# Attention values of the 65 last keys with the operands exchanged: weights stationary, keys moving, and a transpose per head

## The chip, the core and the metric

The kernel runs on one core of a Trainium2 chip. The metric is the device time of one execution in microseconds (us); the median of several runs counts. The engines are called as in the profile: PE (TensorE matmuls) with its weight loads PEld, DVE (VectorE), ACT (ScalarE), POOL (GpSimd) and SP (SyncE, which issues most DMAs). PSUM is the memory that PE writes; it has 8 banks of 128 partitions x 512 f32.

## The reference

A gated cross-attention block and a feed-forward block with eight low-rank experts, all in f32. The change lies in the values `v` of the cross-attention: 4 batches, 256 queries, 1601 keys, 8 key/value heads of 128, 32 query heads.

```python
def _L0_xattn_ref(query, kv, Wq, bq, Wkv, bkv, Wo, bo):
    q = (query @ Wq + bq).reshape(B, L, NKV, G, HDIM)
    k_, v_ = jnp.split(kv @ Wkv + bkv, 2, axis=-1)
    k = k_.reshape(B, Lk, NKV, HDIM)
    v = v_.reshape(B, Lk, NKV, HDIM)
    scores = jnp.einsum('blkgd,bmkd->bkglm', q, k) * scale
    attn = jax.nn.softmax(scores, axis=-1)
    o = jnp.einsum('bkglm,bmkd->blkgd', attn, v).reshape(B, L, NHEAD * HDIM)
    return o @ Wo + bo
...
x = x + jnp.tanh(g_xattn[0]) * _L0_xattn_ref(_layernorm(x, axis=-1), ctx_4096, ...)
x = x + jnp.tanh(g_ffn[0]) * _L0_ffn_ref(_layernorm(x, axis=-1), ...)
```

1601 keys are 12 blocks of 128 and a rest of 65. The 65 are the subject here.

## The kernel before

**Groups and windows.** The work is cut into groups, one for each batch, key/value head and block of 128 queries (`run_group`, L1783). In a group PE makes the scores of 13 key blocks (`score_unit`, L1246, PSUM tile `sc`), which ACT copies to SBUF (L1255), and in between, for the group before, the product of the exponentials with the values (`av_unit`, L1337, tile `av`). DVE folds maxima and sums and subtracts, ACT takes the exponentials (L1285, L1288). Between two groups lies a window (`window`, L1800), in which PE does the other work: queries (`pxq` and the like), keys (`pxk`), values (`pxv`) and output products (`po`, L472, evacuated by ACT at L477).

**The planner.** The order on PE, DVE and ACT is written out by the Python code, which keeps a clock for each of them with a planned cost for each step. A step is a tuple of cost, what it waits for, the function that issues it, and whether it takes a PSUM bank. Steps that must follow each other form a `Task` with a due window. Tasks with a `chain` share `RATE` = 9700 ns of a window by their cost: in L1811, `t.credit = t.cost() * max(min(1, left / max(cost, 1)), 0)`, and a step is taken while half its cost is within the credit. In the window where a task is due its credit is unlimited. Among the steps that may be taken, the one that is ready first goes first (L1822). Between scores, `short_tasks` (L1749) takes steps of up to 4 x 108 ns where they are ready and three banks are free. `act(ns)` adds a piece to ACT's clock and says when its result is there (200 ns for each of the two signals). `bank` takes a PSUM bank from the planner's list, and `give` returns it.

**The values of a pair of heads.** `pair_steps` (L971) makes two heads at once with Strassen-Winograd's seven products, in which the weights' blocks and sums of them (`A11` ... `S4`, 128 x 128 for each `a(slot, c)`) meet blocks of the context and sums of those. For the values, the context is stationary and the weights move (L1015), so that keys come to lie on partitions, as `av` needs them. There are two parts of 384 keys in each half, seven steps of 1344 ns in each part. The 65 keys of the rest do not go through the seven products. `tail` (L1124) makes them directly: for each head `f` four matmuls, with the 65 keys (`cols`, from `tail_cols`) stationary and the weights moving, into 65 partitions x 128 of one bank (`ptv`, L1128); then ACT copies each head's part to block `FULL` of `v_t` (L1136). `tail` is a task of its own beside the two parts, with the same due window and chain. When all steps of the pair are over (`over`, L1141), the weights of the next keys are loaded by SP.

**How often.** 4 batches x 4 pairs of heads, less the first pair, which takes another way: 15 times. Each f32 matmul appears in the trace as two records (each with its weight load), each f32 transpose as one.

**Names of the diff.** `REST` = 65, `P` = `HDIM` = 128, `NC` = 4, `FULL` = 12, `BLOCK_COST` = 224, `TR_COST` = 108 (ns in the plan). `small` is a pool of small SBUF tiles, `ident` the 128 x 128 identity. `banks` and `second` are dictionaries that live as long as the pair's steps; `done` holds the planned time at which a named result is there.

Of the kernel before, what the change touches and what calls it, by code (L numbers as in the profile page):

```python
# [10 lines left out]
F32 = mybir.dt.float32  # L11
# [4 lines left out]
P = 128  # L16
NHEAD = 32
NKV = 8
HDIM = 128
# [8 lines left out]
def flamingo_kernel(  # L28
# [51 lines left out]
    nc = tc.nc  # L80
    B, L, D = x.shape
    LK = ctx_kv.shape[1]
    NC = D // P
# [5 lines left out]
    FULL = KT - 1 if rows[-1] < P else KT  # L89
# [14 lines left out]
    REST = rows[-1] if FULL < KT else 0  # L104
# [8 lines left out]
    small = ctx.enter_context(tc.tile_pool(name="small", bufs=4))  # L113
# [10 lines left out]
    done = {}  # L124
# [7 lines left out]
    def act(ns, ready=None):  # L132
        clock["a"] = max(clock["a"], clock["now"] + SEM if ready is None else ready) + ns
        return clock["a"] + SEM
# [76 lines left out]
    def bank(name):  # L211
        free.remove(min(free))
        return ps.tile([P, 512], F32, tag="bank", name=name)
# [4 lines left out]
    ident = const.tile([P, P], F32, name="ident")  # L218
# [33 lines left out]
    TR_COST = 108  # L252
    BLOCK_COST = 224
# [612 lines left out]
    qT_t, kT_t, v_t = {}, {}, {}  # L866
# [64 lines left out]
    def first_k_steps(b):  # L931

        steps = sum(pair_steps("k", b, 0, lambda: next_weights("v", b, 0)), [])
        return steps
# [36 lines left out]
    def pair_steps(kind, b, hp, then=None):  # L971
# [4 lines left out]
        nm = f"{kind}_{b}_{hp}"  # L976
        h0 = 2 * hp
        banks = {}
        second = {}

        def a(slot, c):
            return w_t[kind, b, hp][:, slot, c, :]
# [130 lines left out]
        def tail_cols(f):  # L1113

            rest, tt = rest_t[b], T_t[b][1]
            if f == 0:
                return [(rest[:, c, :], A11, c) for c in range(2)] + [
                    (rest[:, 2 + c, :], A12, c) for c in range(2)
                ]
            return [(rest[:, c, :], S1, c) for c in range(2)] + [  # L1120
                (tt[:, c, :], A22, c) for c in range(2)
            ]

        def tail():  # L1124
            bk = bank(f"pt{nm}")
            for f in range(2):
                for j, (cols, slot, c) in enumerate(tail_cols(f)):
                    nc.tensor.matmul(  # L1128
                        bk[:REST, f * HDIM : (f + 1) * HDIM],
                        cols,  # L1130
                        a(slot, c),
                        start=j == 0,
                        stop=j == NC - 1,
                    )
            for f in range(2):
                nc.scalar.copy(v_t[b, h0 + f][:REST, FULL], bk[:REST, f * HDIM : (f + 1) * HDIM])  # L1136
                t = act(250)
            give(t)
            over()

        def over():  # L1141
            left[0] -= 1
            if not left[0]:
                done["pair", kind, b, hp] = clock["now"]
                if then is not None:
                    then()
# [12 lines left out]
        parts = [[step(i, s, n) for i in (1, 2, 6, 7, 5, 4, 3)] for s, n in cols]  # L1159
        if REST and not wide:  # L1160
            ready = [("T", "kv", b), ("w", kind, b, hp)]
            parts.append([(2 * NC * BLOCK_COST, ready, tail, True)])
        left = [sum(len(p) for p in parts)]
        return parts

# [688 lines left out]
    def q_steps(b, h, i):  # L1854

        hp = h * NL + i

        def then():

            if (b, hp) == (0, 0):  # L1860
                next_weights("q", 0, 2)
            elif hp + 1 < NHEAD // 2 and (b, hp) != (0, 1):
                next_weights("q", b, hp + 1)

        return pair_steps("q", b, hp, then)[0]
# [110 lines left out]
    for hi, (b, h) in enumerate(heads):  # L1976
        pair, coming = (b, h // 2), next_pair(b, h // 2)
        nxt = heads[hi + 1] if hi + 1 < len(heads) else None
        for l in range(NL):
# [26 lines left out]
            if coming is not None and (h % 2, l) == (0, 1):  # L2006
                cb, cp = coming
                if cb == b:
                    then = lambda c=coming: next_weights("v", *c)
                    steps = sum(pair_steps("k", cb, cp, then), [])  # L2010
                else:
                    steps = first_k_steps(cb)
                tasks.append(Task(steps, (hi | 1) * NL + (NL - 1) * (cb == b), now))
# [66 lines left out]
```

## Time and profile before

| | us |
|---|---|
| median of 3 runs (2532.05 to 2533.65) | 2532.07 |
| the profiled execution's own time | 2532.2 |
| its span, first to last instruction | 2530.4 |
| PE busy in it | 2521.6 |
| DVE busy | 2175.3 |
| ACT busy | 1263.6 |
| `ptv` matmuls, L1128: 180 and 60 records | 22.1 and 9.0 |
| the copies of `ptv`, L1136: 30 | 0.262 each (median) |

A line of groups gives the line of the code, the engine and operation, the tile written and the tiles read, for PE the shape of the stationary operand (rows x columns) and of the result, the number of records, then the busy time, the mean of one in ns and the idle time before them. Records of matmuls overlap, so that busy times of neighbours do not add up; the chain of waits gives each piece its own share. In a matmul's line the first tile read is the moving one and the second the stationary one. A line of the order of time has the start, the length, the engine, the line, the operation and how many records were merged into it.

### The profile page before, as it was taken

What the parts mean: (1) busy time and instruction counts of PE and PEld (TensorE: products, weight loads), DVE (VectorE), ACT (ScalarE), POOL (GpSimd) and SP (SyncE); (2) the same over time, 40 slices, a digit from 0 to 9 for tenths busy, and PEclk for the clock granted to TensorE, in tenths of its full rate; (3) what the DMA queues carried; (4) which work ended last, traced back from release to release, by engine and by line L of the source; (5) the groups of instructions that cost most, each with busy time, mean ns of one, the idle gap of its engine ahead of it and who ended that gap; (6) DMA issues with size and microseconds to landing.
All of it is one profiled execution on the core that took longest, in us unless ns stands there. A gap on an engine that the chain in (4) does not pass through costs nothing.

```text
span 2530.4 us, 27018 instructions
## 1 busy us (share of the span) xinstructions
PE 2521.6 (100%) x9199; PEld 1493.8 (59%) x9199; DVE 2175.3 (86%) x3323; ACT 1263.6 (50%) x2062; POOL 208.8 (8%) x271
## 2 busy tenths in 40 slices
PE   9999999999999999999999999999999999999999
PEld 7557566565555656555665565756656565555544
DVE  4999898898899989999878887878788888889886
ACT  2545454545455554555545454545455455555551
POOL 1000000001001000110010000000000100000100
PEclk9999999999999999999999999999999999999999
DMA  5646857669666543224255535455532222221211
GB/s 170 143 92 130 146 123 118 151 110 246 80 92 99 85 81 74 71 71 152 58 98 100 98 77 96 109 81 110 154 80 65 82 54 67 67 63 44 71 34 50
DMA packets 300136, 246.24 MB, mean 97 GB/s; under 512 B 180533, under 2 KB 256341, under 8 KB 296158
## 3 DMA queue, kind: packets, MB, share of 16 engines
q1 hardware_dynamic: 267278, 211.71, 36.6%
q0 software_dynamic: 32192, 32.55, 8.8%
q8 instruction: 72, 1.18, 0.2%
q14 instruction: 66, 0.54, 0.1%
q10 hardware_dynamic: 528, 0.26, 0.0%
HBM read 147.96 MB, written 96.49 MB: 97 GB/s over the span
## 4 chain that ended last, share of the span: by engine, by line
PE 98%; DVE 1%; DMA 0%; ACT 0%; issue 0%; SPq 0%; ACTq 0%
PE sc L1246 28%; PE av L1337 27%; PE pxv L1015 6%; PE pxk L1004 6%; PE pxq L1004 4%; PE pox L472 4%; PE pyv L1015 3%; PE pyk L1004 3%; PE pyq L1004 2%; PE poy L472 2%; PE pzv L1015 2%; PE pzk L1004 2%; PE pzq L1004 1%; PE ptv L1128 1%; PE poz L472 1%; PE py L1581 1%
## 5 line engine op out<-in xcount | busy, mean ns | idle before, releaser
L1246 PE MATMUL sc<-qT,kT 128*128 128x512 f32 (+1 forms) x1664 | 775.9, 592 | 0.0
L1337 PE MATMUL av<-p,v 65*128 65x512 f32 x1640 | 765.5, 592 | 0.5 <-ACT p L1288 0.5
L1255 ACT COPY p<-sc 65x512 f32<-65x512 f32 x820 | 478.4, 586 | 572.8 <-PE sc L1246 549.0
L1337 PEld LDWEIGHTS av<-p,v 65*128 65x128 f32 x1640 | 311.2, 190 | 384.3 <-issue 380.1
L1246 PEld LDWEIGHTS sc<-qT,kT 128*128 128x128 f32 (+1 forms) x1664 | 308.1, 186 | 375.6 <-issue 349.5
L1285 DVE TENSOR_TENSOR p<-p,mb 65x512 f32<-65x512 f32 x442 | 482.4, 1136 | 0.3
L1288 ACT ACTIVATE p<-p 65x512 f32<-65x512 f32 x442 | 422.3, 990 | 31.0 <-DVE p L1285 29.7
L1181 DVE TENSOR_TENSOR mx<-mx,p 128x1024 f32<-128x1024 f32 x252 | 308.1, 1223 | 146.3 <-ACT p L1255 141.7
L478 POOL DMA_DIRECT2D kept_x<-po x210 | 182.6, 925 | 2039.8 <-ACT po L477 1864.4
L1181 DVE TENSOR_TENSOR sm<-sm,p 128x1024 f32<-128x1024 f32 x252 | 307.6, 1221 | 42.0 <-ACT p L1288 32.0
L1004 PE MATMUL pxq<-xq,wq 128*128 128x256 f32 x512 | 131.2, 379 | 0.0
L1049 ACT ACTIVATE kT<-pxk,biasT 128x384 f32<-128x384 f32 (+1 forms) x120 | 58.1, 509 | 126.5 <-PE pxk L1004 126.0
L1004 PEld LDWEIGHTS pxq<-xq,wq 128*128 128x128 f32 x512 | 92.4, 189 | 32.1 <-issue 15.8
L1049 ACT ACTIVATE qT<-pxq,biasT 128x256 f32<-128x256 f32 x64 | 30.4, 474 | 148.8 <-PE pxq L1004 148.8
L1175 DVE TENSOR_TENSOR mx<-p,p 128x1024 f32<-128x1024 f32 x63 | 76.9, 1221 | 31.6 <-ACT p L1255 31.4
L1004 PE MATMUL pxk<-T,wk 128*128 128x417 f32 (+1 forms) x240 | 90.4, 499 | 0.0
L1015 PE MATMUL pxv<-wv,ctxT 128*128 128x128 f32 x720 | 90.2, 275 | 0.0
L1015 PE MATMUL pxv<-wv,T 128*128 128x128 f32 x720 | 90.2, 275 | 0.0
L1004 PE MATMUL pxk<-ctxT,wk 128*128 128x417 f32 (+1 forms) x240 | 90.0, 499 | 0.0
L1015 PEld LDWEIGHTS pxv<-wv,ctxT 128*128 128x128 f32 x720 | 86.4, 192 | 4.2 <-issue 3.8
L1015 PEld LDWEIGHTS pxv<-wv,T 128*128 128x128 f32 x720 | 86.4, 192 | 4.2 <-issue 3.8
L1052 ACT COPY v<-pxv 128x384 f32<-128x384 f32 x90 | 43.0, 478 | 83.4 <-PE pxv L1015 83.1
(273 smaller groups left out, 2779.5 us busy)
## 6 DMA issues: line engine op xcount, KB each, us to landing
kept_x<-po POOLq DMA_DIRECT2D x210, 128.0 KB, 4.8
wo<-kept_wo SPq DMA_DIRECT2D x22, 1024.0 KB, 7.8
kept_q<-wq SPq DMA_DIRECT2D x16, 896.0 KB, 4.3
wq<-kept_q SPq DMA_DIRECT2D x16, 896.0 KB, 5.1
space<-kept_wo SPq DMA_DIRECT2D x22, 512.0 KB, 3.9
wk<-kept_k SPq DMA_DIRECT2D x11, 896.0 KB, 4.8
wv<-kept_v SPq DMA_DIRECT2D x11, 896.0 KB, 4.6
ctxT<-kept_ctx SPq DMA_DIRECT2D x12, 801.0 KB, 11.8
```

The source lines that it names most:

```text
L472: nc.tensor.matmul(bk[:, :HD], left[i]()[:, c, :], blk[:, c, :], start=first and c == 0, stop=c == 1, skip_group_check=True,)
L478: nc.gpsimd.dma_start(x2_kept[b, l, d], part, accum_op=ALU.add)
L1004: nc.tensor.matmul(bk[:, :n], a(SLOT[i], c), operand(i, c, s, n), start=first and c == 0, stop=c == 1, skip_group_check=True,)
L1015: nc.tensor.matmul(bk[:, t * HDIM : (t + 1) * HDIM], operand(i, c, s + t * P, P), a(SLOT[i], c), start=first and t == 0 and c == 0, stop=c ...
L1049: nc.scalar.activation(dst, src, AF.Identity, bias=bias_of(kind, h0 + f))
L1175: nc.vector.tensor_tensor(acc, p[first], p[first + 1], op)
L1181: nc.vector.tensor_tensor(acc, acc, p[j], op)
L1246: nc.tensor.matmul(sc[:r, :], kT_t[b, h][:, key_col(i) : key_col(i) + r], qT_t[b, h][:, :, l * P : (l + 1) * P], start=True, stop=True,)
L1255: nc.scalar.copy(p[:r, k, :], sc[:r, :])
L1285: nc.vector.tensor_tensor(p, p, m, ALU.subtract)
L1288: nc.scalar.activation(p, p, AF.Exp, scale=scale)
L1337: nc.tensor.matmul(av, v_t[b, h][:r, i, :], p_t[key][j][:r, k, :], start=(j == 0 and k == 0), stop=(j == NPAIR - 1 and k == len(pairs[j]) ...
```

## The change

`tail` exchanges the operands: the weights `a(slot, c)` are stationary and the 65 keys move, so the result has the 128 value features on partitions and 65 keys along the free axis, 130 columns for both heads. ACT copies it to a new SBUF tile of 128 x 130 (`vr`). A second step, `tail_turn`, transposes each head's 128 x 65 on PE into the free half of the same bank, and ACT copies the two results of 65 x 128 to `v_t` as before. The bank is returned after that. In the plan the task now has two steps: 2 x 4 x 124 ns for the product (before 2 x 4 x 224), and 2 x 108 ns for the turn, which waits for the copy.

```diff
         def tail():
-            bk = bank(f"pt{nm}")
+            banks["t"] = bk = bank(f"pt{nm}")
             for f in range(2):
                 for j, (cols, slot, c) in enumerate(tail_cols(f)):
                     nc.tensor.matmul(
-                        bk[:REST, f * HDIM : (f + 1) * HDIM],
+                        bk[:, f * REST : (f + 1) * REST],
+                        a(slot, c),
                         cols,
-                        a(slot, c),
                         start=j == 0,
                         stop=j == NC - 1,
                     )
+            second["t"] = small.tile([P, 2 * REST], F32, tag="vr", name=f"vr_{nm}", bufs=1)
+            nc.scalar.copy(second["t"], bk[:, : 2 * REST])
+            done[nm, "t"] = act(230)
+            over()
+
+        def tail_turn():
+            bk = banks["t"]
             for f in range(2):
-                nc.scalar.copy(v_t[b, h0 + f][:REST, FULL], bk[:REST, f * HDIM : (f + 1) * HDIM])
+                nc.tensor.transpose(
+                    bk[:REST, (2 + f) * HDIM : (3 + f) * HDIM], second["t"][:, f * REST : (f + 1) * REST], ident
+                )
+            for f in range(2):
+                nc.scalar.copy(
+                    v_t[b, h0 + f][:REST, FULL], bk[:REST, (2 + f) * HDIM : (3 + f) * HDIM]
+                )
                 t = act(250)
             give(t)
             over()
...
         if REST and not wide:
             ready = [("T", "kv", b), ("w", kind, b, hp)]
-            parts.append([(2 * NC * BLOCK_COST, ready, tail, True)])
+            parts.append([(2 * NC * 124, ready, tail, True), (2 * TR_COST, (nm, "t"), tail_turn)])
```

## The prediction

> **What bounds the kernel now.** I read the table of engines first, then the chain of work that ended last, then the groups by line with their shapes kept apart, and last the order of time around one of the places that the change touches.
>
> ```profile
> PE 2521.6 (100%) x9199; PEld 1493.8 (59%) x9199; DVE 2175.3 (86%) x3323; ACT 1263.6 (50%) x2062; POOL 208.8 (8%) x271
> ...
> PE 98%; DVE 1%; DMA 0%; ACT 0%; issue 0%; SPq 0%; ACTq 0%
> ```
>
> PE is busy for the whole span and 98% of the chain is PE. What a change does to the time is therefore what it adds to or takes from PE's own stream, at full price, plus any wait that it brings into that stream. The granted clock is 1.00, so rows from different places can be compared.
>
> The chain in order of time shows one place of the change, in the pieces from 244 to 249 us (start, length, what):
>
> ```profile
> 244.19 1.34 PE pyv L1015 x12
> 245.53 1.34 PE pxv L1015 x12
> 246.87 1.75 PE ptv L1128 x16
> 248.62 0.86 PE pox L472 x4
> ```
>
> `ptv` is the product for the last 65 keys of one pair of heads. It has 8 matmuls in the program and 16 records, two for each f32 matmul. It takes 1.75 us, 0.109 us a record. The line occurs 240 times, so there are 15 such places, 26.2 us in all, 1% of the span. No more than that is at stake.
>
> **What a record costs.** Each record is a weight load (PEld) and a matmul (PE). The forms tell which of the two sets the pace:
>
> ```profile
> L1015 PE MATMUL pxv<-wv,ctxT 128*128 128x128 f32 x720 | 90.2, 275 | 0.0
> L1015 PEld LDWEIGHTS pxv<-wv,ctxT 128*128 128x128 f32 x720 | 86.4, 192 | 4.2 <-issue 3.8
> L1128 PEld LDWEIGHTS ptv<-wv,rest 128*65 128x65 f32 x180 | 20.1, 138 | 0.0
> ```
>
> A matmul moves its columns at 0.83 ns a column: the 512-column form lasts 592 ns, the 128-column one 275 (317 ns for 384 columns). A weight load behaves alike: 192 ns for 128 columns against 138 for 65 is 54 ns for 63 columns, 0.86 ns a column. So 128 columns occupy either side for about 107 ns and 65 for about 55. In `pxv` both sides are 128 wide and the pace is 1.34 us / 12 = 0.112 us, not the sum of the two, so load and move overlap and the longer one counts. In `ptv` now the load is 65 wide and the move 128: 0.109 us.
>
> **The swap of the operands.** Afterwards the weights stand (128 columns to load) and the keys move (65). The longer side goes from the move to the load and stays 128 columns wide. No row before has a 65-column move under a 128-column f32 load, so I bound it. The nearest row comes behind four transposes that move 8 columns each, where a score product finds nothing to hide its load:
>
> ```profile
> 2391.61 0.70 PE L1246 MATMUL sc<-qT,kT 128*128 128x512 f32 x1
> ...
> 2391.61 0.30 PEld L1246 LDWEIGHTS sc<-qT,kT 128*128 128x128 f32 x2
> ```
>
> That matmul lasts 0.70 us where its form means 592 ns, 0.105 us more, and two loads of 0.19 end within 0.30 us, so they start 0.11 us apart. A 128-column load that no move covers is paid in full. Under a 65-column move (55 ns) half of it is covered and the pace should be the load's, 0.107 to 0.112 us. I take 0.110: 16 x 0.110 = 1.76 us a place, +0.01 on 1.75. The bounds of this range are -0.04 (0.107) and +0.04 (0.112). The far bound is the four small transposes themselves:
>
> ```profile
> L259 PE MATMUL pt_base<-ident,base 8*128 8x8 f32 x4 | 0.4, 207 | 0.0
> ...
> 2391.27 0.32 PEld L259 LDWEIGHTS pt_base<-ident,base 8*128 8x128 f32 x4 [0.76 <-issue]
> ```
>
> Their loads start (0.32 - 0.14) / 3 = 0.06 us apart. A transpose's load of 128 columns lasts 140 ns, like 65 columns of an ordinary one, which is why this row is not the nearest. If 0.062 held, a place would take 0.99 us, 0.76 less.
>
> The Trainium skill ("TensorE: Matmul & The Clock Gate", LDWEIGHTS) speaks against the change: by it the load goes by its columns, 107 ns for 128, whatever is moved; the swapped product would then take 1.71 us, an estimate, and gain almost nothing. The same page (The mechanism, under packing) has a load overlap a running matmul only where the row groups differ. The 0.112 us of `pxv`, where both use all rows, contradicts this; by that rule load and move would add to 162 ns before and after alike, an estimate, and the product would neither gain nor lose.
>
> **The two transposes.** Each place gains two transposes, with 65 weight columns and 128 moving ones. The chain has the nearest row, between two ordinary products:
>
> ```profile
> 28.30 0.44 PE pt_x L259 x4
> 28.73 3.46 PE pv L955 x16
> ```
>
> 0.44 / 4 = 0.109 us each, and the product behind them keeps its usual 0.216 us a record: a 128-column move covers the next load. 2 x 0.109 = 0.22 us a place. They are single records, so there are no more than 30 of them.
>
> **The copies on ACT.** A copy of 128 x 130 out of PSUM is added, ahead of the two of 65 x 128 (262 ns each now); about 0.27 us, 15 times, 4 us of an engine that is 50% busy. I cost it at nothing. Every time before, the copies start some 0.04 us behind the end of the product's last record, as here (that record ends at 412.90 + 0.60 = 413.50 us):
>
> ```profile
> 413.54 0.42 ACT L1136 COPY v<-ptv 65x128 f32<-65x128 f32 x2 [1.27 <-PE ptv L1128]
> 414.40 0.47 ACT L477 ACTIVATE po<-pox,gates 128x256 f32<-128x256 f32 x1 [0.44 <-PE pox L472]
> ```
>
> ACT stands idle before them and 0.44 us after them. The first added wait is this copy's on the product: behind it in ACT's queue are the evacuations of the output products and the next exponentials. The second is PE's: the transposes wait for the copy, some 0.35 us after the product's end (0.04 and the copy, and a little for the semaphore). What hides it is the planner's rule that a step is taken by when it is ready: the turn counts as ready 630 ns later (200 + 230 + 200), and other steps stand ready, output products of 0.86 us at every one of the 15 places. If that cover were gone, PE would stand for about 0.5 us a place: 0.16 for the product's drain (a record's 273 ns over its pace of 109), 0.04, the copy and its signal. The bank stays held until the turn, some microseconds longer. PE's waits on other engines total only some 5 us in the whole span, so I put that at nothing as well; its price would show as a wait of PE's on an evacuation by ACT.
>
> **The moved step.** The product's planned cost falls from 1792 to 992 ns, 1208 with the turn. The planner gives a chain of steps a share of each window; for the value steps it is 9700 / 20024 = 0.484 (before 9700 / 20608 = 0.471). The product gets 585 ns of credit and needs half its first step, 496, to be taken; before it had 843 and needed 896. So it should move one window earlier, behind the six `pxv`/`pzv` steps, with the turn in that window or among the next scores. PE does the same work. One window grows by 1.8 us and the other, at the shortest 12.9 us (7 value products, the product, two output products), shrinks to 11.1. Windows of 9.5 us (from 787.01 to 796.48 us: six key products, two output products) already pass with no idle PE, so DVE keeps up. The next weights' load on SP is issued when the chain is over, now up to 1.8 us earlier, and it is used 30 us later (issued at 248.65, first product at 278.55 us). No DMA is added; POOL's queue keeps its order.
>
> **Sum.** A place: +0.01 and +0.22 = +0.23 us. 15 places: +3.4 us on the profiled execution's 2532.2 (its span of 2530.4 and 1.8 around it); the median is 2532.07, 0.1 below. Forecast 2535.5 us, 0.13% slower, which is within the 0.2% (5.1 us) that a measurement of this kernel can tell from no change. Its own range is 2532.5 to 2538: the product's bounds give 15 x (-0.04 to +0.04) = -0.6 to +0.6, the shift of windows perhaps 2 either way, judged by PE's stalls of 0.5 to 0.8 us at single places.
>
> **Rivals.** First, the short move sets the pace and the load hides: 0.062 us a record. 15 x (-0.76 + 0.22) = -8.1 us, 2524.0. The pace of the small transposes speaks for it; the uncovered load of 0.105 us and the loads' 0.86 ns a column speak against it. Chance 0.10.
>
> Second, the transposes come before their copy and PE waits: 0.5 us at each place on top of the sum, 15 x (0.23 + 0.5) = +11, 2543. It is slower beyond the limit from 0.11 us of mean wait on (1.7 / 15). For it: PE runs late on its plan, which counts 992 ns for about 1760, and ACT is in order, so an exponential that waits for DVE would hold the copy. Against it: an output product of 0.86 us stands ready at every place. With shorter waits at some places, and with stalls of DVE in the changed windows, chance 0.26, from 2537 to 2543.
>
> Third, that the change does not do what it says, in that the pair's two products are no shorter and the turn costs its 0.22 us, is the forecast itself. Chance 0.64.
>
> **How the numbers follow.** Within 0.2% holds the forecast, less a little at its upper end and with a few gains: 0.62. Slower 0.28, faster 0.10. The range 2531.5 to 2541 leaves out the first rival and the far end of the second.
>
> **What would show it.** The product should take 1.7 to 1.8 us a place in the chain, with weight loads near 190 ns. About 1.0 us would make the first rival right. Thirty transposes of 272 ns must follow an output product or a score, not the product. A group of PE waits on ACT's new copy would be the second rival. A product that still stands behind the last `pxv` would make the moved step wrong, at no cost in time.

## The result, and the profile after

The changed kernel takes 2538.56 us (median of 14 runs, 2536.87 to 2541.15) against 2532.27 (14 runs of the kernel before beside them, 2531.62 to 2535.46): a ratio of 1.0024, 95% interval 1.0016 to 1.0032, 6.3 us slower. The profiled execution took 2539.2 us, its span is 2537.4.

The tables of engines and of the chain, in the page of the changed kernel:

```profile
PE 2526.5 (100%) x9229; PEld 1498.0 (59%) x9229; DVE 2176.3 (86%) x3323; ACT 1264.6 (50%) x2077; POOL 208.7 (8%) x271
...
PE 99%; DVE 0%; ACT 0%; DMA 0%; issue 0%; SPq 0%; ACTq 0%
```

PE has 30 records more, the transposes, and ACT 15, the new copies. PE still sets the end. The first place of the change, in the chain in order of time (start, length, what):

```profile
204.72 1.73 PE ptv L1128 x16
206.46 0.92 PE poy L472 x4
207.38 0.86 PE pox L472 x4
...
212.16 0.22 PE ptv L1143 x2
```

The product takes 1.73 us where it took 1.75, so the swap gained next to nothing. The output product behind it takes 0.92 where its kind takes 0.86 (by the starts of the records it is 0.05 more). The two transposes take 0.22 and stand 5.7 us behind the product's end, between scores (11.6 us at three of the 15 places). The product stands where the plan now takes it, one window earlier (204.72 us, before 246.87). The forms of the groups show why there is no gain (matmuls, then weight loads):

```profile
L1128 PE MATMUL ptv<-rest,wv 128*128 128x65 f32 x180 | 21.8, 271 | 0.0
...
L1128 PEld LDWEIGHTS ptv<-rest,wv 128*128 128x128 f32 x180 | 21.3, 192 | 0.0
```

The loads have grown from 138 to 192 ns. The matmuls move 65 columns and still last 271; that each waits for its load is tested below.

That explains some 4 of the 6.3 us. The rest shows in PE's waits, by what it waited for (total, times, longest in us):

```profile
PE pox L472 <- DVE space L450: 3.0, 1, 3.0
PE warm L1910 <- DVE ones L1907: 1.1, 1, 1.1
PE pt_ctx L259 <- DMA ctx<-in_ctx_dram: 1.0, 1, 1.0
```

One output product waits 3.0 us for DVE's sums (`space`), where the kernel before waits 0.6 us. The wait at `warm` is in the kernel before too. The one on the first load of the context, near the start, comes and goes (a second profile of the changed kernel has none, one of another kernel below 1.2 us) and is no part of the change. In the order of time PE stands at the output product, and what follows is stretched:

```profile
1104.57 1.81 PE L472 MATMUL pox<-space,space 128*128 128x256 f32 x4 [3.03 <-DVE space L450]
1106.18 4.22 PE L1350 MATMUL av<-p,v 128*128 128x512 f32 x7
```

In the kernel before, the same four records last 1.13 us and the seven behind them 3.17 instead of 4.22:

```profile
1100.06 1.13 PE L472 MATMUL pox<-space,space 128*128 128x256 f32 x4 [0.61 <-DVE space L450]
1101.03 3.17 PE L1337 MATMUL av<-p,v 128*128 128x512 f32 x7
```

So 0.7 and 1.05 us, 1.7 in all, are stretching. The table by stretches of the changed kernel (PE, PEld, DVE, ACT and POOL busy, then the granted clock, and last what DMA moved) says what happened:

```profile
1095.00:1101.00 6.00, 6.00 (x16) 2.60 (x14) 5.89 (x9) 1.37 (x3) 0.00 (x0) 1.00 0.01 3
1104.50:1108.50 4.00, 3.93 (x7) 2.29 (x8) 3.53 (x6) 0.47 (x1) 0.90 (x1) 0.57 0.00 0
1109.00:1115.00 6.00, 6.00 (x44) 5.04 (x43) 5.19 (x12) 0.60 (x2) 0.00 (x0) 1.00 0.11 16
```

The granted clock is 0.57 in the 4 us behind the wait and 1.00 before and after them; in single microseconds it is 0.50 from 1105 to 1108 us. The Trainium skill ("TensorE: Matmul & The Clock Gate", the table of goals under "Why this matters for your kernels") says the same: PE should not stand for more than about 3 us. The wait of 3.03 us here was enough; the one of 0.61 before was not.

DVE's order of time shows where the wait comes from. In the kernel before, around this group, whose first score is at 1080.13 us:

```profile
1069.11 0.67 DVE L1193 TENSOR_REDUCE quadm_sm<-sm 128x16 f32<-128x512 f32 x1
...
1081.02 0.23 DVE L1313 RECIPROCAL quadm_sm<-quadm_sm 32x16 f32<-32x16 f32 x1
...
1099.13 0.42 DVE L450 TENSOR_TENSOR space<-oT 128x256 f32<-128x256 f32 x1
```

and in the changed kernel, whose group begins at 1082.21:

```profile
1087.09 0.68 DVE L1206 TENSOR_REDUCE quadm_sm<-sm 128x16 f32<-128x512 f32 x1
...
1098.21 0.23 DVE L1326 RECIPROCAL quadm_sm<-quadm_sm 32x16 f32<-32x16 f32 x1
...
1103.64 0.42 DVE L450 TENSOR_TENSOR space<-oT 128x256 f32<-128x256 f32 x1
```

The end of the earlier group's sums has moved back: the reduction from 11 us ahead of this group's first score to 5 us behind it, the reciprocal from the head of this group's work into its middle. The sums for the output product come 4.5 us later, and 2.1 of these are PE's own delay: DVE is 2.4 us later against PE. The operations are the same; the plan took them in another order.

### The profile page after: what moved, and what is told of

Read it like the earlier page. It is cut to its first block, busy times and chain, and to the rows that moved or that the text cites. A ratio compares the mean times of both kernels' runs of the same rounds, so it can differ in the third digit from the quotient of the medians.

```text
span 2537.4 us, 27121 instructions
## 1 busy us (share of the span) xinstructions
PE 2526.5 (100%) x9229; PEld 1498.0 (59%) x9229; DVE 2176.3 (86%) x3323; ACT 1264.6 (50%) x2077; POOL 208.7 (8%) x271
## 4 chain that ended last, share of the span: by engine, by line
PE 99%; DVE 0%; ACT 0%; DMA 0%; issue 0%; SPq 0%; ACTq 0%
PE av L1350 28%; PE sc L1259 28%; PE pxv L1015 6%; PE pxk L1004 6%; PE pxq L1004 4%; PE pox L472 4%; PE pyv L1015 3%; PE pyk L1004 3%; PE pyq L1004 2%; PE poy L472 2%; PE pzk L1004 2%; PE pzv L1015 2%; PE pzq L1004 1%; PE ptv L1128 1%; PE poz L472 1%; PE py L1594 1%
```

## The experiments

The theory: the 6.3 us are PE's own work at 15 places, about +0.25 us each, and one wait with the clock behind it, brought by the new order. The rivals: all of it is PE's own work, or all of it is the order. All times are medians beside the kernel before on the same chip, with the ratio and its 95% interval.

**The product kept in its old window.** Only the planned costs differ from the changed kernel:

```diff
-            parts.append([(2 * NC * 124, ready, tail, True), (2 * TR_COST, (nm, "t"), tail_turn)])
+            parts.append([(2 * NC * BLOCK_COST, ready, tail, True), (0, (nm, "t"), tail_turn)])
```

> The exchanged product and the transposes stay, but the plan counts the product at 1792 ns as before and the turn at 0, so that the product stays in the window in which it stood before; DVE's order is then nearly that of before. Theory (two parts: PE's own work at each of the 15 places, and a wait of PE on DVE's sums of the output product that comes from the new order): the product takes 1.73 us a place, the two transposes 0.22 and the product behind the exchanged one 0.05 more, so +0.25 us a place, +3.8 in all: 2536.1 us (2535.3 to 2537.0), clock 1.000, and PE's wait on 'space' under 1 us as before. Rival 'all of it is PE's own work': no different from the changed kernel, 2538.5. Rival 'all of it is the order': 2532.3, as before.

2536.02 us against 2532.39, +3.6 (1.0016, interval 1.0007 to 1.0025). The clock in the profile is 1.0 and the wait 0.6 us. This is the change without its shift of windows, and the rival "all of it is the order" falls, since the interval lies above 1. The chain has 1.74 us for the product, 0.92 for the output product behind it and 0.22 for the transposes.

**The plan alone.** The old operands and copies, with the changed kernel's two planned steps; the second one issues the copies:

```diff
-            parts.append([(2 * NC * BLOCK_COST, ready, tail, True)])
+            parts.append([(2 * NC * 124, ready, tail, True), (2 * TR_COST, (nm, "t"), tail_turn)])
```

> The product and the copies of the kernel before (keys stationary, no transposes), in the plan of the changed kernel: a step of 992 ns that is taken one window earlier, and a second one of 216 ns that issues the two copies. DVE's order is that of the changed kernel. Theory (two parts): PE's wait on 'space' near 1100 us grows from 0.8 to about 3 us and the granted clock falls behind it, so +2 to +4 us: 2534.3 to 2536.3. Rival 'all of it is PE's own work': 2532.3. Rival 'all of it is the order': 2538.5.

2536.89 against 2532.39, +4.5 (1.0020, 1.0012 to 1.0029), 0.6 above the theory's upper end. PE waits 3.0 us on `space`, and in its profile 1.9 us more on sums of the queries. A kernel that computes exactly what the one before does, with the same instructions, loses 4.5 us where the change lost 6.3. So the rival "all of it is PE's own work" falls too. Taken alone, this run leaves the order's rival standing (2538.5 is inside the interval); that one fell with the run before.

**Without the transposes**, in the old window:

```diff
-            for f in range(2):
-                nc.tensor.transpose(
-                    bk[:REST, (2 + f) * HDIM : (3 + f) * HDIM], second["t"][:, f * REST : (f + 1) * REST], ident
-                )
...
+                nc.scalar.copy(v_t[b, h0 + f][:REST, FULL], second["t"][:REST, :HDIM])
```

> As the kernel with the product in its old window, but the 30 transposes are left out: the two copies read the untransposed tile, so the values of the 65 last keys are not the reference's. Theory: the transposes cost their 0.109 us each and nothing else, 30 x 0.109 = 3.3 us less than with them, 2532.9 us; what is left over the kernel before is the exposed load behind the product, +0.5 us. Rival (a turn costs more, by a switch between transposes and products or a wait on the copy): 2 us or more below that, or the kernel with the transposes at 2538 and this one at 2533.

2532.97 against 2532.39 (1.0004, 0.9995 to 1.0013), 3.05 us below the kernel with them. The transposes cost 0.10 us each and nothing besides.

**Half the keys moved**, in the old window. The two copies that fill the tile are not shown:

```diff
-                        bk[:, f * REST : (f + 1) * REST],
+                        bk[:, f * 33 : (f + 1) * 33],
                         a(slot, c),
-                        cols,
+                        cols[:, :33],
```

> As the kernel with the product in its old window, but only 33 of the 65 keys move in each matmul; two copies fill the tile with them twice, so the values of the last 32 keys are not the reference's. Theory (the load of 128 columns sets the pace): the product keeps 1.73 us a place, 0.108 us a record. Rival (the move sets the pace, or load and move add): 32 columns less at 0.83 ns are 27 ns a record, 0.43 us a place, 1.3 us a place and 6.4 us less in all.

2537.05 in its one run, 1.0 above the kernel with 65 keys; its profile has a wait of 1.2 us on the first load of the context, which the other's has not. The rival's 6.4 us less did not come. In its chain:

```profile
246.96 1.71 PE ptv L1128 x16
248.67 0.94 PE pox L472 x4
```

With 33 columns the product and the output product behind it take 2.65 us together, with 65 columns 2.66: what moves does not count. What the product saves at its last record (0.03) the next one pays: its second record starts 0.30 us behind its first, with 65 columns 0.27, and in the kernel before 0.22. The less is moved, the less of the load behind it is covered.

**Half the columns loaded**, in the old window, with 65 keys moving. The two copies are again not shown:

```diff
-                        bk[:, f * REST : (f + 1) * REST],
-                        a(slot, c),
+                        bk[:64, f * REST : (f + 1) * REST],
+                        a(slot, c)[:, :64],
```

> As the kernel with the product in its old window, with 65 keys moving, but only 64 of the 128 weight columns are loaded in each matmul; the 64 features of a head are copied twice, so the values of the 65 last keys are not the reference's. Theory (the load sets the pace): both sides are now about 54 ns, so the record falls from 0.108 us to 0.06, the product from 1.73 to about 0.97 us a place, 11 us less in all. Rival (load and move add, or a record has a floor of 0.1 us): no less than 0.1 us a record, 1.6 us a place.

2530.25 in its one run. In its chain:

```profile
246.86 1.08 PE ptv L1128 x16
247.94 1.06 PE pox L472 x4
249.00 0.41 PE ptv L1144 x2
```

The load sets the pace: the product falls from 1.74 to 1.08 us; between its ends the records start 0.059 us apart (median of the trace). I had expected 0.97 and 11 us in all, and it was 5.8. Three things were left out of the sum: the ends of such a run of short records pay for loads that nothing covers (0.09 us at the first record, and 1.06 against 0.92 at the output product behind), and the transposes, which now come sooner behind two copies, wait for ACT (0.41 here instead of 0.22). By the starts of the records that delays them by 0.2 to 0.5 us at five places, 1.7 in all. The chain's 0.66 less for the product and 0.14 more behind it make 0.52 us a place, 7.8 in all; less the 1.7 it is 6.1, near the 5.8 of this one run.

**One product's window.** Of the 15 products, the one of batch 1, pair 2 alone decides whether the plan has DVE's old order or the new one near the long wait. So the changed kernel with the old plan for it alone, and the reverse:

```diff
+            old = (b, hp) == (1, 2)
-            parts.append([(2 * NC * 124, ready, tail, True), (2 * TR_COST, (nm, "t"), tail_turn)])
+            parts.append([(2 * NC * (BLOCK_COST if old else 124), ready, tail, True), (0 if old else 2 * TR_COST, (nm, "t"), tail_turn)])
```

> The changed kernel, in whose plan one of the 15 products alone, that of batch 1 and pair 2, has its old cost and so its old window; the work of all engines is the same. DVE's order ahead of the output product near 1115 us is then that of the kernel before. Theory (that order is what PE waits 3.0 us for): the wait is back at 0.6 to 0.8 us and the granted clock at 1.000 in every run. What is left is +3.8 us of PE's own work, less about 1 us of waits on exponentials near 2460 us that the new order avoids: 2535.2 us (2534.3 to 2536.2). Rival (the wait comes of the later arrival of PE or of the extra work, wherever the steps stand): 2538.5 us with the wait.

2536.46 against 2532.73, +3.7 (1.0015, 1.0005 to 1.0024), so about 2.6 of the change's 6.3 us go with this one step. The wait is back at 0.6 us. The clock is 1.000 in the profile; one of the runs had 0.999. The time is above the expected 2535.2: a wait of 1.1 us on sums of the queries near 322 us takes most of what the order saves near 2460 us. Only kernels with the new order in the first batches have that wait, and not each of their profiles.

The reverse has `old = (b, hp) != (1, 2)`:

> The reverse: the exchanged product and the transposes everywhere, the old plan for 14 products, the new one for that of batch 1 and pair 2 alone. Theory: the wait of 3.0 us near 1115 us and the lower clock behind it come back from this one step, so +2.2 us of wait and 0 to 3 us of clock on the 2536.0 of the kernel with all products in their old windows: 2538.2 to 2540. Rival (it takes the whole new order): 2536.0, clock 1.000.

2540.52 against 2532.73, +7.8 (1.0032, 1.0020 to 1.0044). The wait of 3.0 us is there and every run has a clock of 0.999. Against the kernel with all products in the old window (+3.6) that is 4.2 us for one step of the plan. I expected 2.2 to 4 of wait and clock; it is just above the upper end. The traces account for it: the wait is 2.4 us longer (3.03 against 0.61), and the clock is at half for 3.4 us, which costs 1.7.

**The wait filled.** The changed kernel with idle work on PE in the place of the wait:

```diff
+                if (b, h, i) == (1, 4, 6):
+                    fill = bank("fill")
+                    for n in range(12):
+                        nc.tensor.matmul(fill[:, :P], ident, ident, start=True, stop=True)
+                    give(clock["now"])
```

> The changed kernel, with 12 matmuls of the identity with itself (24 records, 2.6 us) put on PE ahead of the one output product that waits 3.0 us for DVE's sums; nobody reads them. They fill the wait and move nothing else. Theory (of the time behind the wait a part is the clock, which falls since PE stands): the records behind the wait keep their usual lengths, the granted clock is 1.000 in every run, PE's wait is under 0.7 us, and the time is 1 to 2 us below the changed kernel on the same chip, about 2537.0, with less spread. Rival (the clock has no part, or falls for another reason): no different from the changed kernel.

> The changed kernel once more, beside the others of this call. All theories: 2538.5 us, spread from 2536.9 to 2541.

Filled, 2538.76 us (2537.93 to 2539.73, 10 runs, all with a clock of 1.000); unfilled on the same chip, 2539.65 (2537.89 to 2541.07, clock from 0.998 to 1.000). The order of time of the filled kernel:

```profile
1102.19 2.84 PE L474 MATMUL fill<-ident 128*128 128x128 f32 x24
1105.39 1.13 PE L477 MATMUL pox<-space,space 128*128 128x256 f32 x4 [0.35 <-DVE space L450]
```

The output product lasts 1.13 us again, as it does before the change, so the stretching was the clock, and the clock fell since PE stood. The medians differ by 0.9 us, less than the 1 to 2 expected, and the times overlap, so that they alone would not show it. The spread falls from 3.2 to 1.8 us. One reason for the small difference is that only three of these eight unfilled executions show a clock under 1.000. In the first 14 executions of the changed kernel ten do, at 2538.1 to 2541.2 us; of the four with 1.000, three took 2536.9 to 2537.0 and one 2540.3. Both kernels were 1 to 2 us slower here than the first runs of the changed kernel had led me to expect, and both have a wait of 1.0 us on sums of the queries in their profiles. Why that one comes and goes between executions was not tried.

**A version meant to be faster than both.** The product of before, in the new plan for batch 1 and pair 2 excepted:

> The product of the kernel before (keys stationary, no transposes) in the plan of the changed kernel, but for batch 1 and pair 2. Theory: no wait of 3 us, none of the exchanged product's cost, and the waits near 2460 us avoided: 2531.3 us, 1 us below the kernel before, at the edge of what can be told. Rival (the new plan costs elsewhere too, as its wait on the queries' sums of 1.9 us in the earlier profile): 2533 or more.

2532.70 against 2532.73 (1.0000, 0.9991 to 1.0009): the order elsewhere gains and loses the same, again with a wait of 1.2 us on sums of the queries. The waits that the new order avoids near 2460 us stand in the kernel before as

```profile
2460.64 1.12 PE L1337 MATMUL av<-p,v 65*128 65x512 f32 x2 [0.46 <-ACT p L1288]
2462.20 10.57 PE L1337 MATMUL av<-p_last,v 128*128 128x512 f32 x24 [0.44 <-ACT p_last L1288]
```

And with the new plan for batches 2 and 3 alone (`old = b < 2`):

> The product of the kernel before (keys stationary, no transposes), in the new plan for the products of batches 2 and 3 alone. Theory: neither the wait near 1115 us nor the one on the queries' sums, but the two waits on exponentials near 2460 us are avoided, 1.4 us: 2531.0 us. Rival (the order of these batches has other waits): 2532.4 or more.

2531.13 against 2532.63 (0.9995, 0.9986 to 1.0004), 1.5 us less in the median, as expected, but not clear of the measurement. Its trace shows the gain: from the `av` at the head of this stretch to the feed-forward product behind it 25.8 us pass, in the changed kernel too, and 27.2 in the kernel before.

## Why the prediction was right, and where it was not

**The sum.** Forecast were 2535.5 us, 0.13% slower; measured are 2538.56, 0.24% (0.16 to 0.32), on the forecast's side of the kernel before, but 3 us above it. It is inside the full range (2531.5 to 2541) and outside the sum's own (2532.5 to 2538). That the range reached so far is partly luck: its upper part was given to the second rival, mainly for transposes that wait for their copy, which did not come; only its "stalls of DVE in the changed windows" did. The parts: +3.6 us of PE's own work (+3.4 predicted), +4.2 for one step in another window (0 predicted), and some -1.5 for waits near 2460 us that the new order avoids (not foreseen): 6.3, as measured. The three come from different kernels, so that the agreement is better than their intervals allow. The one step is worth 4.2 us alone, 2.6 by leaving it out of the changed kernel, and 4.5 with the old product (4.5 with it, 0 without); the wait on the queries' sums is one thing that differs between them.

**The swap.** Right. The pace is the load's: 0.108 us a record, as bounded, against 0.110 chosen. Fewer columns moved changed nothing and fewer columns loaded changed it at once. Missed was the far end of the product: its last short move covers only half of the next load, 0.05 us a place, so that the swap costs 0.04 us a place rather than 0.01.

**The transposes.** Right: 0.22 us a place predicted and seen in the chain, 3.05 us in all by leaving them out.

**The copies and the bank.** Right. No transpose waits for its copy in the changed kernel, and none of PE's waits there is on a copy of the product's bank. The second rival, the transposes ahead of their copy, did not come.

**The moved step.** Its place was right, its cost was not. This is the term that failed: "PE does the same work", "so DVE keeps up", put at nothing with 2 us either way for the shift. It cost 2.7 (6.3 less 3.6). I had asked whether the shorter windows leave DVE enough time, and they do. But the plan also decides the order of DVE's pieces by the clock that the step moves. At one group, in which DVE also prepares the queries' inputs of the next two batches, the other order put 2.4 us more ahead of sums that PE needs. A wait of 0.61 us became 3.03, and the clock then fell. That it would be slower beyond 0.2% had a chance of 0.28, for waits of this kind among others; the likeliest case did not hold.

**The first rival**, the short move setting the pace, is refuted by the run with 33 keys.

## What to carry to other kernels

Exchanging a matmul's operands for fewer moving columns gained nothing here, because the load of the weights was the longer side afterwards: look at the weight loads' durations by their width, and compare the larger of load and move before and after. When a planned cost changes, the work that the planner places elsewhere has changed too: run the new plan with the old instructions, which here lost 4.5 us by itself where the whole change lost 6.3. An engine that is full at one stage sets the price of such a move, whatever its mean share is: DVE is busy for 86% of the span, but for 5.9 of the 6 us ahead of the long wait.

## What the runs showed of the hardware

The number of moved columns drops out where the load is longer: 65 or 33 columns under a load of 128 made the same 2.65 us with the product behind. Loads of 64 columns under 65 moving ones run at 0.059 us a record. In all four traces with a stand of PE of 3.0 us the granted clock falls to 0.50, in three for 3.4 us and in one (the plan alone) for 6.8. The moment differs between executions of the same kernel: 0.3 us behind the end of the stand in one profile of the changed kernel, 0.4 us ahead of it in the other. In the filled kernel, where PE stood 0.35 us, the clock was 1.000 in all ten runs.
